# Residual added in PSUM in one unit of fifteen in place of one in six, with a new order of the work: a Restormer block on one Trainium2 core

## The chip, the cores and the metric

The kernel runs on one core of one Trainium2 chip. Its engines are TensorE (PE in the profile, with its weight loads as PEld), VectorE (DVE), ScalarE (ACT), GpSimd (POOL) and SyncE (SP, which issues DMAs). Each works through its own list of instructions in a fixed order, and waits on semaphores for what others make. The metric is the time of one execution on the device in microseconds; of the kernel before there are three timed runs and one profiled execution.

## The reference: what is computed

All numbers are float32. An input of 16 images, 128 channels, 96 x 96 pixels, goes through an attention across channels and a feed-forward part with a 3x3 depthwise convolution, each behind a layer norm and each added to what went in. Cut to what matters:

```python
B, C, H, W = (16, 128, 96, 96); HID = 4 * C; HEADS = 8
def _attention(xn, wq, wk, wv, wp):       # attention of channels on channels, 8 heads of 16
    q, k, v = split(xn @ wq.T), split(xn @ wk.T), split(xn @ wv.T)
    attn = softmax(einsum('bhcn,bhdn->bhcd', l2norm(q), l2norm(k)) * HEAD_DIM ** -0.5)
    ...
    return out @ wp.T
def _ffn(xn, w_in, w_dw, w_out):
    h1 = einsum('bchw,oc->bohw', xn, w_in[:, :, 0, 0])        # 128 -> 512 channels
    h2 = depthwise 3x3 convolution of h1 with w_dw, padding 1
    return einsum('bchw,oc->bohw', gelu(h2), w_out[:, :, 0, 0])
x = x + attn_out                                   # first residual
x = x + _ffn(layernorm(x) over channels, ...)      # second residual: this change is about it
```

## The kernel before, in words

**Tiling.** An image is cut into 8 bands of 12 rows (1152 pixels), a band into 3 units of 4 rows (384 pixels), so that there are 128 bands, counted `g` = 0 to 127, and 384 units. Channels lie on the 128 partitions. An image passes through three stages, and the program runs the first stage of one image, the second of the image before and the feed-forward part at the same time.

- Stage a (norm 1): PE transposes x to pixels on partitions (`forth`, L2072), ACT copies that to a tile `zT` (L2109), DVE takes mean and variance (`stats`, L2080), POOL makes 1/sqrt from them in two small steps (`variance` L2085, `power` L2089) and scales zT with it (`scaled`, L2113). PE sums the Gram matrix over the whole image (L2120) and transposes back to channels (L2168). A chain of small steps turns the Gram matrix into one 128 x 128 matrix for the image.
- Stage b: PE applies that matrix (`mix`, L2022), ACT brings it out of PSUM (L2031), a DMA adds x to it (L2034). Transposes, statistics and `variance`/`power` follow as above, and DVE writes the normalised `xn` (L2172).
- Feed-forward part: for each band the 512 hidden channels are four chunks `n` of 128; a band and chunk together are a job, named (g, n). PE makes the hidden values (`hidden`, L2366) and ACT copies them to SBUF (`kept`, L2371). Of the nine taps of the depthwise convolution ACT makes two to four as separate products (L2382); POOL adds one of these and the middle tap into the tile `merged` (L2385, a second one at L2388); DVE runs the rest as a chain of multiply-adds. The chain begins with a **first tap** that reads `h` and `merged`, both in SBUF (written acc<-h,ratio,merged, L2394), goes on in PSUM (L2398), and ends in the SBUF tile `h3` (h<-h,ratio,acc, L2394). DMAs issued by POOL add the other products on top (L2407, L2410), and ACT applies gelu (L2415). For 45 of the 128 bands the fourth chunk is done by PE alone, as nine matmuls (L2478).
- Output: for each unit PE multiplies the four chunks with `woutT` into one PSUM bank (L2518, two matmul records for each product, since float32 goes through in two passes), the residual x is added, and SP stores the band (L2532).

**The residual.** It is added in one of two ways. Where `in_psum` holds, PE first multiplies x by the identity into the same bank (L2517) and ACT copies the finished sum to SBUF (L2526). Elsewhere DVE adds the bank and x (L2528). `SUM_OF, SUM_AT = 2, 1` says where: unit 1 of every second band, 64 units of 384.

**What sets the order.** `Plan` collects some 18,900 operations with a cost and a due time each; `order()` runs a list scheduler over them, and then moves single operations by hand-searched steps: in `MOVES`, each engine has a table "the operation at place n goes m places later or earlier". So the order on each engine is fixed before the program is built. `in_turn()` replays the lists with a model of durations, to write all engines' operations into one program and to give out buffers. The four PSUM banks `h`, the tiles `zT`, `pr`, `h3`, and the batches of statistics go round among their users; an operation that takes a buffer waits for the last user of it. The replay's times are not on the chip: only its order and its choice of buffers are.

**One port.** The replay treats the first tap on DVE and POOL's `merge` and `scaled` (marked `two`) as taking turns at one port to SBUF.

Of the kernel before, what the change touches and what calls it, by code (L numbers as in the profile page):

```python
# [49 lines left out]
SUM_OF, SUM_AT = 2, 1  # L50
# [164 lines left out]
    PE={6: -1, 11: -1, 13: -1, 18: 0, 19: -3, 26: -1, 28: -1, 29: 7, 33: -3, 37: 3, 38: 6, 39: -4, 44: -2, 47: -2,  # L215
        48: -2, 50: -3, 53: 0, 54: -2, 56: -1, 58: -1, 60: 8, 64: -2, 66: 5, 68: -2, 70: -5, 72: -2, 76: -1,
        78: -1, 84: -1, 88: -1, 90: 0, 91: -2, 95: -1, 102: -7, 105: 0, 106: 5, 107: 7, 108: 1, 110: 6, 111: -9,
        118: -1, 120: 4, 122: -3, 124: -3, 126: 3, 129: 4, 130: -5, 132: 3, 134: 4, 135: -4, 137: 5, 139: 5,
        142: -3, 144: 2, 148: 3, 149: -2, 151: 4, 157: 2, 159: 3, 161: 7, 162: 3, 167: 2, 170: 6, 171: 2, 176: -4,
        177: 2, 179: -5, 180: -3, 185: 2, 194: -3, 196: 7, 197: 5, 199: 9, 200: -22, 203: -23, 204: 7, 206: -23,  # L220
        211: 1, 213: -3, 214: -7, 215: -1, 217: 4, 219: 14, 220: 3, 221: 1, 222: 9, 230: 6, 233: 4, 234: 7, 235: 0,
        238: 1, 239: 9, 241: 9, 242: -8, 243: 2, 246: 12, 250: 4, 254: 18, 255: -31, 256: -30, 257: -28, 258: -28,
        259: -27, 260: -22, 261: -21, 262: -20, 263: -11, 264: -11, 265: -10, 266: -7, 267: -11, 268: -11, 269: -9,
        271: -7, 272: -7, 274: 0, 275: 5, 278: -8, 279: 3, 281: 11, 282: -6, 283: -20, 284: 9, 285: 26, 286: 12,
        287: -18, 288: -15, 289: 24, 290: -19, 294: -15, 295: 2, 296: -15, 297: -9, 298: 17, 301: 17, 305: -1,
        306: -6, 307: 22, 314: -7, 316: -8, 317: -5, 318: 25, 321: 3, 326: 7, 328: -12, 329: 30, 330: 5, 331: -14,
        332: 10, 333: -12, 334: 32, 335: -9, 336: 9, 337: 25, 338: -10, 340: 23, 341: -4, 342: -11, 347: -8,
        348: -1, 349: 15, 356: -1, 357: 10, 358: 10, 359: 11, 360: 9, 361: 11, 362: -14, 363: -13, 371: 17,
        372: -7, 373: -15, 375: -14, 377: 4, 378: 32, 381: 33, 382: -2, 387: 5, 388: -5, 389: -5, 390: -8, 397: 3,
        398: 8, 400: -6, 401: -4, 402: -7, 408: -6, 409: -5, 413: -2, 415: 0, 416: -4, 417: 6, 418: 6, 420: 7,  # L230
        424: -3, 427: 13, 429: -13, 430: 5, 437: 7, 438: 5, 442: -8, 443: -7, 444: -7, 445: 5, 450: 7, 451: 5,
        452: -14, 454: -23, 455: -13, 456: -23, 457: -9, 458: 1, 460: -8, 461: 1, 473: -1, 474: 4, 475: 2, 476: -2,
        477: 37, 478: 37, 479: 6, 480: -1, 481: 35, 484: 33, 486: 4, 487: 6, 488: 6, 491: -3, 496: -1, 498: 5,
        499: 5, 500: -4, 503: 4, 504: 16, 505: 19, 507: 14, 509: 19, 510: 19, 513: 19, 514: 33, 515: -83, 516: -56,
        517: -41, 518: -45, 519: -11, 521: -39, 528: -6, 529: 2, 530: -4, 532: 9, 533: 1, 536: 4, 548: 3, 549: -44,
        550: -41, 552: -27, 554: 12, 555: -44, 557: 1, 558: -5, 560: 2, 561: 8, 562: -7, 563: -9, 565: 13,
        566: -10, 567: -2, 570: 7, 576: 19, 577: 10, 580: 10, 582: 3, 585: -3, 586: -2, 587: -11, 588: -2, 589: 3,
        590: 6, 593: 6, 595: -15, 596: -15, 597: -34, 598: -24, 600: -17, 601: -28, 602: 7, 603: -42, 605: -26,
        606: 8, 608: 8, 609: 8, 610: -8, 614: 4, 616: 9, 618: 23, 620: 8, 621: 2, 624: 0, 633: 0, 636: -1, 637: 0,
        644: 11, 645: 12, 646: 15, 648: 14, 649: 15, 650: 17, 651: 14, 654: 14, 656: 16, 658: 16, 659: -1, 660: 18,  # L240
        661: -57, 662: 8, 663: -31, 666: -18, 668: -12, 670: -17, 671: -21, 673: 7, 675: -4, 676: 30, 677: 32,
        678: 34, 679: 38, 682: -3, 688: 34, 689: -38, 690: 34, 697: 3, 698: 0, 700: -12, 702: 26, 703: 13,
        705: -11, 706: 23, 707: 25, 708: 2, 709: -8, 710: -56, 711: 7, 712: -35, 713: -24, 715: -11, 716: -17,
        717: -14, 719: -12, 720: 0, 727: -8, 730: -4, 733: 5, 734: 3, 735: 4, 740: -5, 749: -3, 750: -1, 751: 5,
        753: 4, 754: 0, 758: 5, 759: 20, 760: 4, 766: -4, 768: -3, 770: -2, 774: -1, 776: 9, 777: 9, 778: 2,
        781: 8, 782: 8, 783: 0, 784: -7, 785: 17, 792: 4, 793: -5, 794: -3, 797: -37, 798: 29, 799: 4, 800: 20,
        801: 0, 802: 5, 804: 0, 810: -4, 813: -4, 815: 2, 817: -7, 818: -5, 819: -7, 820: -4, 821: -6, 822: -8,
        827: 9, 829: -1, 830: 11, 831: 15, 832: -1, 836: 1, 840: -18, 841: 2, 842: -18, 843: -1, 845: -16, 846: -1,
        847: -14, 849: 2, 856: 8, 860: 7, 861: 1, 862: 3, 864: 5, 867: 3, 868: 5, 870: 8, 876: 11, 877: 2, 880: 0,
        883: 5, 885: 5, 887: -38, 888: -38, 889: -41, 890: -29, 891: -34, 892: -26, 893: -1, 896: -2, 897: -1,  # L250
        898: 4, 899: 5, 906: -3, 907: -7, 908: -1, 909: -4, 910: 19, 913: -3, 920: 3, 921: 5, 922: -5, 926: -2,
        930: 0, 934: 0, 942: -5, 945: -6, 947: -5, 948: 4, 949: 10, 950: 3, 951: -37, 953: -2, 955: -17, 957: 18,
        959: -18, 960: 21, 961: 2, 965: 3, 966: 28, 967: -24, 968: 19, 970: -20, 978: -1, 979: 19, 982: -18,
        983: -7, 984: -6, 987: -22, 988: -22, 989: -19, 990: -18, 991: 16, 992: -25, 993: -22, 994: -21, 995: -9,
        996: -22, 997: 4, 998: -10, 999: -20, 1000: 0, 1001: -21, 1002: -20, 1003: 3, 1004: 4, 1005: -22, 1006: 6,
        1007: 4, 1008: 6, 1009: 18, 1010: 10, 1011: 18, 1012: 26, 1013: 26, 1014: 14, 1015: -2, 1016: 1, 1017: 23,
        1018: 25, 1021: 23, 1023: -2, 1024: 23, 1025: 24, 1026: 26, 1027: 6, 1028: 6, 1029: 8, 1030: 23, 1043: -1,
        1044: -19, 1045: -14, 1046: 0, 1048: 36, 1049: 13, 1051: 14, 1053: 46, 1054: 25, 1055: -1, 1056: 24,
        1057: 26, 1060: 27, 1063: -12, 1065: -10, 1068: 21, 1069: -13, 1070: 21, 1071: 21, 1072: -11, 1074: 22,
        1075: -16, 1077: 20, 1079: -22, 1080: 20, 1081: -23, 1083: 18, 1086: -19, 1087: -18, 1089: -19, 1090: -17,  # L260
        1091: 19, 1092: 11, 1093: 12, 1095: -23, 1096: -20, 1097: 12, 1098: -13, 1100: 6, 1101: -24, 1102: -24,
        1103: -28, 1104: -23, 1105: 12, 1106: 8, 1110: 6, 1111: 7, 1112: 8, 1113: 10, 1114: 8, 1115: 20, 1116: 21,
        1117: 7, 1119: 6, 1121: 21, 1122: -9, 1123: 3, 1130: 23, 1132: -5, 1134: -1, 1136: 20, 1140: -2, 1141: -5,
        1142: 50, 1143: 57, 1144: 57, 1145: -13, 1146: -3, 1147: 15, 1148: 16, 1149: 75, 1150: 15, 1151: 64,
        1152: -5, 1153: 65, 1154: -5, 1158: -1, 1168: 8, 1169: 10, 1170: 11, 1173: -21, 1176: -9, 1177: -22,
        1178: -27, 1179: -10, 1180: -10, 1181: -23, 1182: -28, 1183: -11, 1185: 46, 1186: 10, 1187: 12, 1188: 14,
        1190: -10, 1192: -1, 1193: 2, 1194: 52, 1195: -34, 1196: -25, 1197: -24, 1198: -16, 1201: -15, 1202: -13,
        1203: -15, 1204: 22, 1205: 24, 1208: 24, 1209: 18, 1211: 64, 1212: -15, 1215: 22, 1216: 22, 1217: 11,
        1218: -15, 1220: -11, 1221: -10, 1224: 6, 1230: 20, 1231: -17, 1235: 17, 1238: -17, 1240: -18, 1241: -18,
        1243: 20, 1244: -9, 1245: -3, 1247: 33, 1251: 20, 1252: 44, 1253: 44, 1254: 45, 1256: 20, 1257: 24,  # L270
        1258: 42, 1259: 42, 1260: -16, 1262: -14, 1263: 40, 1264: -17, 1265: -7, 1266: -9, 1267: 39, 1268: -9,
        1269: -9, 1275: -7, 1278: -11, 1284: -11, 1285: 22, 1287: -15, 1288: 5, 1289: 20, 1293: -14, 1294: -10,
        1295: -1, 1296: -14, 1299: 31, 1302: -14, 1306: -15, 1307: 9, 1308: 0, 1314: -3, 1316: 1, 1317: -27,
        1318: -26, 1323: -28, 1325: 2, 1326: -28, 1328: -2, 1329: -25, 1330: -28, 1335: -6, 1338: 12, 1339: -5,
        1341: -5, 1342: -5, 1343: -5, 1344: 17, 1345: -17, 1346: 19, 1347: -16, 1348: 11, 1349: 28, 1350: 12,
        1351: -18, 1352: -9, 1353: -9, 1354: -8, 1355: -16, 1356: -16, 1357: 22, 1358: 22, 1359: 23, 1360: 23,
# [2334 lines left out]
```

## Time and profile before

| | |
|---|---|
| timed runs | 3909.78, 3913.20 and 3914.52 us; median 3913.2 |
| profiled execution, its own time | 3910.02 us |
| its span, first to last instruction | 3908.1 us |
| busy, PE / DVE / ACT / POOL | 3852.1 / 3807.1 / 3636.3 / 3370.3 us |
| weight loads, PEld | 2502.7 us |
| granted TensorE clock | 1.000 |

Busy times count an engine's instructions once where they overlap; issuing instructions and waits are not counted. In rows of groups come line, engine, operation, tile written <- tiles read, shape and count, then busy time and the mean of one in ns, then the idle time of the engine just before them and what ended it. In rows of the timeline come start and duration in us, and idle time before the row in brackets.

### The profile page before, as it was taken

To read this page: it belongs to the slowest core of one execution; us is meant where nothing else is said; L and a number is where in the kernel's file an instruction comes from. 1 tells how busy PE (TensorE), PEld (TensorE's weight loads), DVE (VectorE), ACT (ScalarE), POOL (GpSimd) and SP (SyncE) were. 2 spreads that over 40 slices of the span, in tenths; PEclk is the share of its full clock that TensorE was granted. 3 is DMA by queue.
4 is the path that set the end of the run, shared out by engine and by line. 5 is a ranking of instruction groups with operands and counts; after the bars stand their busy time and mean duration, and the time that the engine had idled before them with its cause. 6 is when DMAs were issued, how large, how long until landed. Compare 5 with 4: busy or idle time off the path is not lost.

```text
span 3908.1 us, 50778 instructions
## 1 busy us (share of the span) xinstructions
PE 3852.1 (99%) x16595; PEld 2502.7 (64%) x16595; DVE 3807.1 (97%) x4328; ACT 3636.3 (93%) x5542; POOL 3370.3 (86%) x3107
## 2 busy tenths in 40 slices
PE   8999999999999999999999999999999999999999
PEld 7666666666666666666666666666666666666555
DVE  7999999999999999999999999999999999999998
ACT  3999999999999999999999999999999999999996
POOL 5998888888898888989889899898998889888784
PEclk9999999999999999999999999999999999999999
DMA  3999999999999999999999999999999999999996
GB/s 99 191 206 213 196 209 204 209 200 201 200 200 204 206 192 210 200 210 210 192 204 204 202 210 201 206 200 212 206 204 199 210 211 189 213 207 187 203 192 146
DMA packets 191689, 777.39 MB, mean 199 GB/s; under 512 B 22208, under 2 KB 23616, under 8 KB 191424
## 3 DMA queue, kind: packets, MB, share of 16 engines
q0 software_dynamic: 151920, 622.33, 83.9%
q1 hardware_dynamic: 38784, 151.75, 10.7%
q8 instruction: 131, 2.15, 0.2%
q14 instruction: 134, 1.10, 0.1%
q10 hardware_dynamic: 720, 0.07, 0.0%
HBM read 148.85 MB, written 75.50 MB: 57 GB/s over the span
## 4 chain that ended last, share of the span: by engine, by line
PE 38%; DVE 5%; ACT 3%; POOL 2%; issue 1%; DMA 1%; POOLq 0%; DVEq 0%; ACTq 0%
PE h L2518 11%; PE h L2366 9%; PE h L2478 8%; PE h L2022 2%; PE h L2168 2%; PE g L2120 2%; PE h L2072 2%; DVE acc L2398 2%; ACT pr L2382 1%; DVE acc L2394 1%; DVE h L2394 1%; POOL merged L2385 1%; ACT h L2415 1%; ACT h L2371 1%; DMA h<-pr 1%
## 5 line engine op out<-in xcount | busy, mean ns | idle before, releaser
L2382 ACT ACTIVATE pr<-h,ratio 128x1152 f32<-128x1152 f32 x1494 | 1847.7, 1267 | 17.8 <-DMA h<-pr 5.5
L2398 DVE SCALAR_TENSOR_TENSOR acc<-h,ratio,acc 128x1152 f32<-128x1152 f32 (+1 forms) x1308 | 1809.7, 1384 | 11.3
L2385 POOL TENSOR_TENSOR merged<-pr,h 128x1152 f32<-128x1152 f32 x466 | 1207.8, 2592 | 110.2 <-DVE acc L2394 56.8
L2518 PE MATMUL h<-h,woutT 128*128 128x384 f32 x3072 | 1115.2, 486 | 1.9 <-ACT h L2492 1.2
L2366 PE MATMUL h<-xn,winT 128*128 128x384 f32 (+2 forms) x2802 | 1097.8, 494 | 14.0 <-DVE x L2528 3.7
L2478 PE MATMUL h<-xn,comp 128*128 128x380 f32 (+2 forms) x2430 | 902.8, 482 | 0.1
L2518 PEld LDWEIGHTS h<-h,woutT 128*128 128x128 f32 x3072 | 563.1, 189 | 353.6 <-issue 13.3
L2371 ACT COPY h<-h 128x384 f32<-128x384 f32 (+2 forms) x1401 | 658.3, 493 | 81.8 <-PE h L2366 76.1
L2394 DVE SCALAR_TENSOR_TENSOR acc<-h,ratio,merged 128x1152 f32<-128x1152 f32 x466 | 684.1, 1468 | 15.6 <-POOL merged L2388 7.9
L2366 PEld LDWEIGHTS h<-xn,winT 128*128 128x128 f32 x2802 | 495.9, 190 | 309.4 <-issue 22.6
L2394 DVE SCALAR_TENSOR_TENSOR h<-h,ratio,acc 128x1152 f32<-128x1152 f32 x467 | 655.4, 1403 | 5.9
L2410 POOL DMA_DIRECT2D h<-pr x466 | 475.0, 1030 | 175.7 <-PE h L2518 23.5
L2415 ACT ACTIVATE h<-h,ksum 128x1152 f32<-128x1152 f32 (+1 forms) x586 | 611.9, 1070 | 13.1 <-DMA h<-pr 12.4
L2478 PEld LDWEIGHTS h<-xn,comp 128*128 128x128 f32 x2430 | 429.5, 189 | 223.4 <-issue 14.3
L2407 POOL DMA_DIRECT2D pr<-pr x466 | 469.6, 1026 | 74.9 <-ACT pr L2382 58.7
L2089 POOL TENSOR_TENSOR ve_b<-ve_b,mhalf 128x4 f32<-128x4 f32 x288 | 356.5, 1256 | 10.7
L2072 PEld LDWEIGHTS h<-ident,x 128*128 128x128 f32 x2244 | 270.5, 141 | 134.1 <-issue 57.8
L2089 POOL TENSOR_TENSOR ve_a<-ve_a,mhalf 128x4 f32<-128x4 f32 x288 | 346.5, 1208 | 10.5
L2113 POOL TENSOR_TENSOR zT<-zT,ve_a 128x512 f32<-128x512 f32 x270 | 344.2, 1283 | 5.8
L2072 PE MATMUL h<-ident,x 128*128 128x128 f32 x2244 | 331.5, 274 | 9.7 <-DMA x<-in_x_dram 2.4
L2022 PE MATMUL h<-xn,mwT 128*128 128x384 f32 x768 | 296.5, 489 | 5.2 <-DVE st_b L2080 1.9
L2120 PEld LDWEIGHTS g<-zT 128*128 128x128 f32 x2160 | 273.1, 191 | 42.7 <-POOL zT L2113 4.6
(190 smaller groups left out, 3940.2 us busy)
## 6 DMA issues: line engine op xcount, KB each, us to landing
pr<-pr POOLq DMA_DIRECT2D x466, 576.0 KB, 7.1
h<-pr POOLq DMA_DIRECT2D x466, 576.0 KB, 7.6
x<-in_x_dram SPq DMA_DIRECT2D x128, 576.0 KB, 6.5
out_dram<-x SPq DMA_DIRECT2D x127, 576.0 KB, 4.6
x<-in_x_dram POOLq DMA_DIRECT2D x123, 576.0 KB, 7.7
out_dram<-x SPq DMA_DIRECT2D x3, 192.0 KB, 1.9
h<-in_L_conv_w_in_dram SPq DMA_DIRECT2D x1, 256.0 KB, 3.3
h<-in_L_conv_w_out_dram SPq DMA_DIRECT2D x1, 256.0 KB, 3.7
```

Source lines behind the costliest of these rows:

```text
L2072: nc.tensor.transpose(d["pT", q][:, k, :], xt[:, j * P : (j + 1) * P], ident)
L2089: nc.gpsimd.tensor_tensor(rstd, rstd, mhalf, ALU.pow)
L2366: nc.tensor.matmul(rows(ph), lhsT=winT[:, n, :], rhs=window(xn, r0 + r, e - r, 1), start=True, stop=True)
L2371: nc.scalar.copy(window(h1_, r, e - r, 1), rows(d.pop(("ph", r))))
L2382: nc.scalar.activation(to, shifted(t), AF.Copy, scale=ratio[:, n, t : t + 1])
L2385: nc.gpsimd.tensor_tensor(merged, d["pr", dma_taps[0]], shifted(UNIT), ALU.add)
L2394: nc.vector.scalar_tensor_tensor(to, shifted(t), ratio[:, n, t : t + 1], also, ALU.mult, ALU.add)
L2398: nc.vector.scalar_tensor_tensor(to, shifted(t)[:, lo:hi, cut], ratio[:, n, t : t + 1], to, ALU.mult, ALU.add)
L2410: nc.gpsimd.dma_start(out=h3_of(g, n), in_=d["pr", dma_taps[1]], accum_op=ALU.add)
L2415: nc.scalar.activation(h3, h3, AF.Gelu, bias=ksum[:, z, n : n + 1])
L2478: nc.tensor.matmul(d["pc"][:, lo:hi, cut], lhsT=comp[:, t, :], rhs=window(xn, r0 + dy, UR, dx)[:, lo:hi, cut], start=(t == order[0]), stop ...
L2518: nc.tensor.matmul(rows(d["po"]), lhsT=woutT[:, n, :], rhs=h3s[g, n][:, s * UR : (s + 1) * UR, :], start=(k == 0 and not in_psum), stop=(k ...
```

## The change

Three things change.

1. `SUM_OF` goes from 2 to 5. `in_psum` now holds for unit 1 of every fifth band: 26 units in place of 64. Of the 64, 13 stay; 51 go to DVE's add, and 13 others go from DVE to PE and ACT. Net, 38 units lose the identity product on PE and the copy on ACT, and get an add on DVE.
2. `in_turn()` has more of a model: after a DMA issue POOL's next results come later (`LAG`, `ISSUED`), and a first tap on DVE that comes within `RACE` of certain starts on POOL lets a POOL operation with a port turn go ahead of it. `PE_RATE` goes from 0.989 to 1.002.
3. Nearly every row of `MOVES` is new. Counted over the operations that stay on their engine, 66% of PE's, 37% of DVE's, 73% of ACT's and 61% of POOL's stand at another place; the median of the shift is one place or none, and nine in ten move by at most two to four.

```diff
-SUM_OF, SUM_AT = 2, 1
+SUM_OF, SUM_AT = 5, 1
...
-    PE={6: -1, 11: -1, 13: -1, 18: 0, 19: -3, 26: -1, 28: -1, 29: 7, 33: -3, 37: 3, 38: 6, 39: -4, 44: -2, 47: -2,
...
-PE_RATE, SPARE = 0.989, 75
+PE_RATE, SPARE, LAG, ISSUED, RACE, AHEAD = 1.002, 75, 300, 250, 940, 560
...
         dma = port = taken = 0.0
+        lag, behind = 0, -RACE
...
                     if e == "POOL" and not ops[k][8]:
                         time = max(time, taken)
+                    if e == "DVE" and ops[k][9] and time < behind + RACE and head["POOL"] < len(lists["POOL"]):
+                        other = lists["POOL"][head["POOL"]]
+                        if ops[other][9]:
+                            if times.get("POOL") is None:
+                                times["POOL"] = ready(other, "POOL")
+                            if times["POOL"] is not None and times["POOL"] <= min(time + AHEAD, free_at["POOL"] + 40):
+                                time = max(time, times["POOL"] + 1)
...
             if engine == "POOL":
                 last_pool = None if queue else k
+                straight = time < free_at["POOL"] + 40
+                behind = time if queue else time + ns - 600 if straight and two else -RACE
+                lag = 2 if queue else lag if straight else 0
+                if queue:
+                    ns -= ISSUED
+                elif lag:
+                    result += LAG * lag / 2
+                    lag -= 1
```

The changed file has 7 lines more ahead of the functions, so that each line number above is 7 higher in it (L2528 is L2535 there).

**First place: DVE, band 62** (band 6 of image 7; x_7_6 is its residual). The add of unit 1 was not on DVE; rows run in DVE's order. Before:

```order
L2394 SCALAR_TENSOR_TENSOR h_1_154<-h_2_142,ratio,acc 128x1152
L2528 TENSOR_TENSOR x_7_6_12661<-h_76,x_7_6_12661 128x384
L2394 SCALAR_TENSOR_TENSOR acc<-h_3_143,ratio,merged 128x1152
L2172 TENSOR_TENSOR xn<-x_8_1_13295,h_74 128x4x96
L2398 SCALAR_TENSOR_TENSOR acc<-h_3_143,ratio,acc 128x1056
L2080 BN_STATS st_a_8_13593<-zT_161 128x6
L2398 SCALAR_TENSOR_TENSOR acc<-h_3_143,ratio,acc 128x1056
L2528 TENSOR_TENSOR x_7_6_12661<-h_76,x_7_6_12661 128x384
L2398 SCALAR_TENSOR_TENSOR acc<-h_3_143,ratio,acc 128x1056
```

The same place on DVE in the changed kernel:

```order
L2401 SCALAR_TENSOR_TENSOR h_1_154<-h_2_142,ratio,acc 128x1152
L2535 TENSOR_TENSOR x_7_6_12644<-h_73,x_7_6_12644 128x384
L2401 SCALAR_TENSOR_TENSOR acc<-h_3_143,ratio,merged 128x1152
L2405 SCALAR_TENSOR_TENSOR acc<-h_3_143,ratio,acc 128x1056
L2535 TENSOR_TENSOR x_7_6_12644<-h_76,x_7_6_12644 128x384
L2405 SCALAR_TENSOR_TENSOR acc<-h_3_143,ratio,acc 128x1056
L2535 TENSOR_TENSOR x_7_6_12644<-h_75,x_7_6_12644 128x384
L2179 TENSOR_TENSOR xn<-x_8_1_13283,h_73 128x4x96
L2405 SCALAR_TENSOR_TENSOR acc<-h_3_143,ratio,acc 128x1056
```

Two adds of this band have become three, between the taps of one chain, and the write of xn stands later.

**Second place: POOL, band 76** (the job that begins image 9's fifth band; ve_a is the 1/sqrt of stage a, merged<-pr,h the merge). Before, in POOL's order:

```order
L2385 TENSOR_TENSOR merged<-pr_151,h_0_140 128x1152
L2388 TENSOR_TENSOR merged<-merged,pr_149 128x1152
L2085 TENSOR_SCALAR ve_a_0_15994<-st_a_0_15944 128x4
L2407 DMA pr_150<-pr_145 128x1152
L2113 TENSOR_TENSOR zT_164<-zT_164,ve_a_17_15969 128x4x128
L2089 TENSOR_TENSOR ve_a_0_15994<-ve_a_0_15994,mhalf 128x4
L2385 TENSOR_TENSOR merged<-pr_151,h_1_141 128x1152
```

The same place on POOL in the changed kernel:

```order
L2092 TENSOR_SCALAR ve_a_0_15944<-st_a_0_15929 128x4
L2392 TENSOR_TENSOR merged<-pr_145,h_0_140 128x1152
L2120 TENSOR_TENSOR zT_164<-zT_164,ve_a_17_15922 128x4x128
L2395 TENSOR_TENSOR merged<-merged,pr_150 128x1152
L2096 TENSOR_TENSOR ve_a_0_15944<-ve_a_0_15944,mhalf 128x4
L2392 TENSOR_TENSOR merged<-pr_152,h_1_141 128x1152
```

The scaling of zT stood behind both merges and a DMA issue; it now stands between the two merges, and the DMA issue has gone further back.

More of the change, by code (lines that the diff above doesn't have):

```diff
@@ L214 @@
 MOVES = dict(
-    PE={6: -1, 11: -1, 13: -1, 18: 0, 19: -3, 26: -1, 28: -1, 29: 7, 33: -3, 37: 3, 38: 6, 39: -4, 44: -2, 47: -2,
[320 rows of a table removed]
-    DVE={2: -1, 8: 0, 9: -2, 12: -1, 16: -1, 18: -1, 19: 2, 24: -2, 32: 0, 34: 5, 36: 6, 37: -6, 38: -2, 40: -5,
[161 rows of a table removed]
-    ACT={5: -1, 7: -1, 9: 3, 12: -2, 13: 3, 16: 5, 20: -1, 22: -4, 25: 2, 33: -2, 39: -1, 41: 2, 42: 3, 43: 5,
[275 rows of a table removed]
-    POOL={0: 5, 2: 4, 4: 5, 5: 18, 6: 5, 7: 19, 18: -3, 21: -3, 28: -1, 30: -2, 32: -1, 38: 0, 40: -4, 42: -3,
[147 rows of a table removed]
-    SP={8: -5, 17: -1, 20: -1, 22: -1, 24: -1, 30: -1, 32: -1, 34: -1, 37: -2, 40: -1, 44: -1, 46: -1, 50: -1,
[4 rows of a table removed]
@@ L1127 @@
-    h={18: -1, 23: 1, 24: -1, 25: -3, 28: -1, 30: 7, 33: -2, 36: 0, 37: -2, 38: -4, 40: -2, 43: -1, 48: -1,
[164 rows of a table removed]
-    x1={22: -1},
-    h3={0: 6, 15: -1, 26: -1, 38: -1, 49: -1, 73: -1, 85: -2, 97: -2, 120: -1, 134: -1, 145: -1, 158: -1, 168: -1,
-        181: -2, 193: -1, 205: -1, 218: -1, 231: -3, 241: -1, 254: -1, 265: -1, 278: -1, 290: -2, 313: -2, 327: -3,
-        337: -1, 348: -1, 361: -1, 373: -1, 386: -1, 396: -1, 409: -1, 469: -1, 480: -1, 492: -1, 502: -1, 507: -2,
-        514: 2, 520: -1},
+    PE={3: -3, 10: 3, 12: -5, 16: 3, 19: -2, 21: 7, 26: -2, 27: 3, 29: 6, 32: 4, 33: -8, 38: 6, 39: 1, 40: -1,
[320 rows of a table added]
@@ new lines @@
+    DVE={2: 0, 4: 1, 5: -5, 7: -3, 9: -1, 11: -1, 14: 0, 16: 0, 19: -6, 21: -1, 29: -1, 31: 3, 35: 1, 37: -6, 39: 0,
[160 rows of a table added]
+    ACT={2: -2, 5: -2, 6: -2, 9: -1, 14: -1, 16: 6, 19: -1, 22: -1, 24: -8, 25: 2, 29: 4, 32: -1, 33: -4, 39: -1,
[269 rows of a table added]
+    POOL={2: 4, 4: 4, 5: 21, 6: 5, 7: 21, 9: -7, 11: -7, 13: -4, 20: -5, 30: -1, 32: -2, 37: 4, 39: 3, 41: 2, 43: 2,
[144 rows of a table added]
+    SP={1: -1, 5: 0, 7: 0, 8: -6, 17: -1, 20: -1, 22: -1, 36: 0, 37: -2, 46: -1, 48: -1, 52: -1, 57: 0, 58: -2,
[3 rows of a table added]
+    h={4: -1, 6: 3, 10: -3, 14: 1, 15: -4, 17: -3, 22: -2, 23: 3, 28: -1, 30: 8, 33: -1, 35: 4, 36: -3, 40: 0,
[166 rows of a table added]
@@ L1297 @@
+    x1={1: -1, 4: -1, 22: -1},
+    xb={1: -1},
+    h3={2: -1, 4: -2, 6: -1, 15: -2, 26: -1, 38: -1, 73: -1, 85: -2, 96: -1, 109: -1, 134: -1, 145: -1, 168: -1,
+        181: -2, 193: -2, 205: -1, 231: -3, 254: -1, 265: -1, 278: -2, 289: -1, 301: -1, 313: -2, 327: -3, 337: -2,
+        361: -2, 373: -1, 386: -1, 409: -1, 480: -1, 492: -2, 502: -2, 515: -1, 519: -1},
 )
 ISSUE, FROM_POOL, PORT = dict(DMA=500, DVE=480, ACT=240), 170, 126
-PE_RATE, SPARE = 0.989, 75
+PE_RATE, SPARE, LAG, ISSUED, RACE, AHEAD = 1.002, 75, 300, 250, 940, 560
```

2133 rows, old and new, of tables (ACT, DVE, PE, POOL) are left out of this document.

## The prediction

> **What bounds the kernel now.** I read the page's first part, then the stretches of the span, then the waits of the fullest engine, and last the timeline where a term has to be priced.
>
> ```profile
> PE 3852.1 (99%) x16595; PEld 2502.7 (64%) x16595; DVE 3807.1 (97%) x4328; ACT 3636.3 (93%) x5542; POOL 3370.3 (86%) x3107
> PE 38%; DVE 5%; ACT 3%; POOL 2%; issue 1%; DMA 1%; POOLq 0%; DVEq 0%; ACTq 0%
> ```
>
> Two engines are nearly full: PE, with 3908.1 - 3852.1 = 56.0 us idle, and DVE, with 101.0 us. The chain that ended last names PE far more than DVE. The change takes work from the first and gives work to the second, so the question is how much room DVE has. The stretches tell where its idle time lies (after the stretch come PE, PEld, DVE, ACT and POOL, busy us and instructions):
>
> ```profile
> 0.00:100.00 100.00, 88.21 (x580) 71.86 (x581) 74.54 (x190) 36.39 (x73) 58.52 (x113) 1.00 0.35 102
> 100.00:3850.00 3750.00, 3709.37 (x15845) 2398.50 (x15844) 3693.07 (x4105) 3572.99 (x5420) 3299.76 (x2985) 1.00 0.97 203
> 3850.00:3909.00 59.00, 54.55 (x173) 32.34 (x171) 39.51 (x35) 26.90 (x50) 12.05 (x11) 1.00 0.52 121
> ```
>
> Of DVE's 101.0 us, 25.5 lie in the first 100 us, 18.6 after 3850, and 56.9 in the 3750 us between. There DVE is 98.5% busy and PE 98.9%: both bound it, each waiting a little for the other.
>
> The end cannot give much:
>
> ```profile
> 3886.19 1.42 DVE L2394 SCALAR_TENSOR_TENSOR h<-h,ratio,acc 128x1152 f32<-128x1152 f32 x1
> ...
> 3903.94 1.20 DVE L2528 TENSOR_TENSOR x<-h,x 128x384 f32<-128x384 f32 x2 [9.90 <-PE h L2518]
> ```
>
> DVE's last tap ends at 3887.6, and 20.5 us follow in which PE finishes the output. In the order, 24 products on PE stand from the first that needs this last tap to the end, before and after the change alike. So I take those 20.5 us as fixed: the end comes when DVE has got through its taps, plus 20.5. PE's saving reaches the end only through DVE's waits.
>
> **The change part by part.** All sums are made against the profiled execution's own time, 3910.0 us (span 3908.1, 1.9 around it). It is 3.2 below the median of the three runs and inside their range.
>
> *Work moved, 38 units net.* What one unit costs on each engine:
>
> ```profile
> 1999.19 0.81 PE L2517 MATMUL h<-x,ident 128*128 128x384 f32 x2
> 1999.84 1.45 PE L2518 MATMUL h<-h,woutT 128*128 128x384 f32 x4
> ...
> L2526 ACT COPY x<-h 128x384 f32<-128x384 f32 x64 | 30.9, 483 | 3.6 <-PE h L2518 3.3
> ...
> 2004.14 0.55 DVE L2528 TENSOR_TENSOR x<-h,x 128x384 f32<-128x384 f32 x1
> 2004.61 1.42 DVE L2394 SCALAR_TENSOR_TENSOR acc<-h,ratio,merged 128x1152 f32<-128x1152 f32 x1
> ```
>
> Records overlap, so I take the distance from one start to the next. PE: 0.65 us for the two identity records, 38 x 0.65 = **24.7 us less**. ACT: 38 x 0.483 = 18.4 us less; ACT has 272 us idle, so this counts for nothing. DVE: 0.47 us for an add, 38 x 0.47 = **17.9 us more**, and with DVE 98.5% full nothing hides it.
>
> An add on DVE also adds a wait: the taps queued behind it stand still until PE has finished the unit, and PE gets the bank back from DVE in place of ACT. Rows of the middle stretch price both:
>
> ```profile
> L2528 DVE TENSOR_TENSOR x<-h,x 128x384 f32<-128x384 f32 x311 | 170.8, 549 | 5.3 <-PE h L2518 4.1 <-issue 0.4
> L2366 PE MATMUL h<-xn,winT 128*128 128x384 f32 (+2 forms) x2758 | 1080.6, 494 | 13.8 <-DVE x L2528 3.7 <-DVE xn L2172 3.1 <-ACT h L2371 1.7
> ```
>
> 5.3 us for 311 adds makes 0.65 for 38, and 3.7 on PE makes 0.45; I leave both out. The band's store on SP waits for the add wherever it is made, so no queue but DVE's is passed.
>
> *Port turns.* First taps read `h` and `merged`, both in SBUF; last taps of the same size read PSUM for one of the two:
>
> ```profile
> L2394 DVE SCALAR_TENSOR_TENSOR acc<-h,ratio,merged 128x1152 f32<-128x1152 f32 x461 | 676.7, 1468 | 15.2 <-POOL merged L2388 7.9 <-POOL merged L2385 5.3
> L2394 DVE SCALAR_TENSOR_TENSOR h<-h,ratio,acc 128x1152 f32<-128x1152 f32 x461 | 646.9, 1403 | 5.8
> ```
>
> The difference, 676.7 - 646.9 = 29.8 us, is time in which first taps stand still. It sits in few of them. 21 took over 1.65 us; these are the longest, the shortest, and one that shows with POOL's rows how it comes about:
>
> ```profile
> 1003.86 4.20 DVE L2394 SCALAR_TENSOR_TENSOR acc<-h,ratio,merged 128x1152 f32<-128x1152 f32 x1
> 2876.86 1.67 DVE L2394 SCALAR_TENSOR_TENSOR acc<-h,ratio,merged 128x1152 f32<-128x1152 f32 x1
> ...
> 2370.58 0.91 POOL L2407 DMA_DIRECT2D pr<-pr  x1
> 2371.23 1.34 POOL L2113 TENSOR_TENSOR zT<-zT,ve_a 128x512 f32<-128x512 f32 x1
> 2372.24 2.42 POOL L2089 TENSOR_TENSOR ve_a<-ve_a,mhalf 128x4 f32<-128x4 f32 x1
> ...
> 2370.84 2.96 DVE L2394 SCALAR_TENSOR_TENSOR acc<-h,ratio,merged 128x1152 f32<-128x1152 f32 x1
> ```
>
> While POOL issued a DMA (2370.58) the tap started (2370.84), the scaling of zT got in first all the same, and the tap took 2.96 us in place of some 1.40. The new order takes this scaling away from there (second place above): it runs between the two merges, for which the tap has to wait anyway. In 20 of the 21 a scaling stood on POOL behind the tap's own last merge, straight or with small steps between, or behind a DMA issue that follows that merge. In the new order 4 of the 20 have lost this pattern and 16 keep it; whether those still collide hangs on a few hundred ns, which no order shows. Over the whole list, 85 scalings stand straight behind a DMA issue, and 82 did before, so new losses can arise. Bounds: 0 and 29.8 us. The 4 places alone would make 4/20 of 29.8, 6.0; a list that moved at six places in ten on POOL should shift others too. I take half, **14.9 us less**.
>
> *Waits of DVE in the middle.* The longest, of the 56.9 us:
>
> ```profile
> DVE xn L2172 <- PE h L2168: 8.2, 15, 1.8
> DVE acc L2394 <- POOL merged L2388: 7.9, 7, 3.0
> DVE acc L2394 <- POOL merged L2385: 5.3, 9, 1.4
> DVE x L2528 <- PE h L2518: 4.1, 11, 0.8
> DVE st_b L2080 <- PE h L2072: 3.8, 8, 0.9
> ```
>
> 16.1 us are waits for PE, 13.2 for POOL's merge. PE gets 24.7 us of room, so its results come earlier against DVE's list: between 0 and 16.1, I take 10. The merge comes late where it stands behind a DMA issue or a port turn; the replay now reckons with that, but 265 merges stand straight behind a DMA issue where 230 did. Between 0 and 13.2, I take half, 6.6. The other 27.6 us of DVE's idle time are gaps of well under a microsecond, and I leave them. Nothing excludes that a new order makes new waits; the rivals price that.
>
> **The sum.** 3910.0 + 17.9 - 14.9 - 10 - 6.6 = **3896.4 us**, 13.6 less than now. PE then has 24.7 - 13.6 = 11.1 us more idle time than now, which fits an engine that is no longer the first bound. With nothing regained it is 3910.0 + 17.9 = 3927.9; with all three terms in full (59.1 together), 3910.0 + 17.9 - 29.8 - 16.1 - 13.2 = 3868.8.
>
> **The rivals.**
>
> *DVE alone is the bound, and the new order wins nothing (slower).* DVE pays 17.9 us in the middle stretch, its port losses only move to other taps, and PE waits longer: 3927.9 us. It comes out slower by over 0.2% (above 3921.0 against the median) when less than 7 us come back of the 59.1 that could. For it: DVE has just 56.9 us idle in 3750, and as many scalings stand behind DMA issues as before. Against it: the chain that ended last follows PE for 38% of the span and DVE for 5%. The Trainium skill has a rule by which this rival would be the rule: Perfetto Trace Analysis, section "Identifying the Most-Contended Engine", says that the busy share of matmuls is no measure of how near the limit PE is, and that the share of the weight loads is to be taken instead. By that, PE stands at 64% and DVE at 97%, the work taken from PE is worth nothing, and the sum is 3927.9 less whatever the order regains. This trace does not bear the rule out in full:
>
> ```profile
> 2363.88 3.23 PE h L2518 x10
> ```
>
> Ten records start 0.32 us apart here, and the 0.65 us from one unit's identity product to its next record is the same pace: PE does not idle behind its 64%. Chance 0.17.
>
> *The order wins about what the adds cost.* Between 7 and 23 of the 59.1 us come back and the time is near 3911 (3905 to 3921). This is also the case in which the table does not do what its model says, since the replay is a model and only its order reaches the chip. Chance 0.23.
>
> *PE was the bound.* Then its saving comes through in full, 3910.0 - 24.7 = 3885.3 us, and port turns that are won come on top as far as DVE's list allows: near 3877 (3869 to 3885). For it: PE's share of the chain, and PE idle only 40.6 us in the middle. Against it: DVE would have to regain 51 of its 59.1 us. Chance 0.16.
>
> **How the numbers follow.** The forecast, some half of DVE's losses regained (3885 to 3905), has 0.44; the three rivals have, in their order, 0.17, 0.23 and 0.16. A measurement of this kernel can tell about 0.2% from no change, that is 7.8 us at 3913.2: faster is below 3905.4, slower above 3921.0. So faster 0.44 + 0.16 = 0.60, same 0.23, slower 0.17. The range runs from 3873 to 3922: it takes in the forecast, the case of no change and the first of the slower one, and most of the case in which PE was the bound. It leaves out some 0.15 above and 0.04 below.
>
> **What would show it.** In the changed profile: the identity products x52, DVE's adds x358 and ACT's copies x26; DVE's busy time at 3807.1 + 17.9 - 14.9 = 3810 us and PE's some 3840 (its records overlap, and it stays close to full); the mean of first taps near 1435 ns where it is 1468; waits of DVE for PE in the middle near 6 us and for the merge near 7; DVE's last tap some 14 us earlier, and still about 20 us from there to the end. The prediction is wrong if first taps still average 1468 or more, if DVE's idle time in the middle stays at 57 us or grows, or if the 20 us of the end change.

## The result, and the profile after

| | before | after |
|---|---|---|
| timed runs, median | 3911.5 us (4 runs, 3907.9 to 3914.5) | 3938.3 us (4 runs, 3934.0 to 3942.3) |
| ratio, 95% interval | | 1.0069 [1.0051, 1.0086] |
| profiled execution, its own time | 3910.0 us | 3942.3 us |
| DVE idle in the middle stretch | 56.9 us | 76.9 us |
| PE idle in the middle stretch | 40.6 us | 70.9 us |

The change makes the kernel 26.8 us slower. The forecast was 3896.4 us, 41.9 below the measured time, and the measured time lies above the range of 3873 to 3922. The first part and the chain of the page after:

```profile
PE 3855.6 (98%) x16519; PEld 2482.2 (63%) x16519; DVE 3819.4 (97%) x4366; ACT 3625.7 (92%) x5504; POOL 3414.2 (87%) x3107
PE 38%; DVE 14%; POOL 10%; issue 5%; ACT 3%; DMA 2%; POOLq 0%; DVEq 0%; ACTq 0%
```

GpSimd (POOL) executes the same 3107 instructions as before, is busy 43.9 us longer, and its share of the chain goes from 2% to 10%. The stretches follow, with the columns as before. The program grew by 32 us, so the middle stretch is taken 30 us longer and the last one 2 us:

```profile
0.00:100.00 100.00, 89.60 (x584) 72.27 (x585) 73.75 (x189) 35.61 (x70) 55.93 (x112) 1.00 0.35 100
100.00:3880.00 3780.00, 3709.08 (x15760) 2376.47 (x15759) 3703.15 (x4142) 3560.69 (x5382) 3344.34 (x2985) 1.00 0.96 201
3880.00:3941.00 61.00, 56.93 (x180) 33.48 (x178) 42.49 (x37) 29.43 (x54) 13.98 (x11) 1.00 0.58 131
```

The loss is in the middle: DVE's idle time there is 3780.0 - 3703.15 = 76.9 us, PE's 3780.0 - 3709.08 = 70.9 us. PE has 76 records less to work through and is idle longer. The last tap and the last add show that the end is as it was:

```profile
3919.01 1.41 DVE L2401 SCALAR_TENSOR_TENSOR h<-h,ratio,acc 128x1152 f32<-128x1152 f32 x1
...
3937.03 0.56 DVE L2535 TENSOR_TENSOR x<-h,x 128x384 f32<-128x384 f32 x1 [0.66 <-PE h L2525]
```

The last tap ends at 3920.4, 32.8 us later than before, and 20.2 us follow where 20.5 did. The counts are as the change says (PE shows two records for each of the 26 identity products):

```profile
L2524 PE MATMUL h<-x,ident 128*128 128x384 f32 x52 | 21.0, 485 | 0.0
L2533 ACT COPY x<-h 128x384 f32<-128x384 f32 x26 | 12.4, 477 | 4.1 <-PE h L2525 4.1
L2535 DVE TENSOR_TENSOR x<-h,x 128x384 f32<-128x384 f32 x358 | 197.2, 552 | 19.1 <-PE h L2525 18.5
```

Next, taps of the middle stretch, and under them DVE's longest waits in it:

```profile
L2401 DVE SCALAR_TENSOR_TENSOR acc<-h,ratio,merged 128x1152 f32<-128x1152 f32 x461 | 671.1, 1456 | 26.3 <-POOL merged L2392 13.5 <-POOL merged L2395 10.6
L2401 DVE SCALAR_TENSOR_TENSOR h<-h,ratio,acc 128x1152 f32<-128x1152 f32 x461 | 648.6, 1407 | 5.7
```

```profile
DVE acc L2401 <- POOL merged L2392: 13.5, 18, 2.2
DVE xn L2179 <- PE h L2175: 11.3, 17, 1.8
DVE acc L2401 <- POOL merged L2395: 10.6, 11, 2.2
DVE st_b L2087 <- PE h L2079: 7.3, 10, 2.4
DVE x L2535 <- PE h L2525: 4.6, 4, 2.2
```

First taps lose 671.1 - 648.6 = 22.5 us in place of 29.8. DVE waits 24.1 us for the merge in place of 13.2, and in the three rows for PE 4.6 + 11.3 + 7.3 = 23.2 in place of 16.1. Put into the prediction's sum that makes 3910.0 + 17.9 - 7.3 + 7.1 + 10.9 = 3938.6, near the 3942.3 of this execution. But such a sum only says where DVE stood still; what made it stand still is for the runs to tell.

GpSimd's own groups, before and then after:

```profile
L2385 POOL TENSOR_TENSOR merged<-pr,h 128x1152 f32<-128x1152 f32 x466 | 1207.8, 2592 | 110.2 <-DVE acc L2394 56.8 <-ACT pr L2382 38.3 <-ACT h L2415 4.6
L2089 POOL TENSOR_TENSOR ve_b<-ve_b,mhalf 128x4 f32<-128x4 f32 x288 | 356.5, 1256 | 10.7
L2089 POOL TENSOR_TENSOR ve_a<-ve_a,mhalf 128x4 f32<-128x4 f32 x288 | 346.5, 1208 | 10.5
```

```profile
L2392 POOL TENSOR_TENSOR merged<-pr,h 128x1152 f32<-128x1152 f32 x466 | 1255.9, 2695 | 111.6 <-DVE acc L2401 56.3 <-ACT pr L2389 43.7 <-ACT h L2378 2.6
L2096 POOL TENSOR_TENSOR ve_a<-ve_a,mhalf 128x4 f32<-128x4 f32 x288 | 393.0, 1368 | 8.9
L2096 POOL TENSOR_TENSOR ve_b<-ve_b,mhalf 128x4 f32<-128x4 f32 x288 | 379.4, 1333 | 9.8
```

The same instructions take longer: `power` 772.4 us in place of 703.0, the first merge 1255.9 in place of 1207.8. Of the 48 us more in the merge, some 42 lie in merges that start without a gap behind a DMA issue of GpSimd. By the two traces these are 108 before, of 2.80 us on average, and 165 after, of 2.92; a merge that starts behind a pause lasts 2.43 in both. And PE waits longer for `power` (`ve_b`) and for the scaling (`zT`), here before and then after:

```profile
PEld h L2168 <- POOL ve_b L2089: 10.3, 20, 1.8
PEld g L2120 <- POOL zT L2113: 4.6, 9, 1.2
PE h L2168 <- POOL ve_b L2089: 2.2, 4, 1.3
```

```profile
PEld h L2175 <- POOL ve_b L2096: 25.3, 36, 2.3
PEld g L2127 <- POOL zT L2120: 11.5, 17, 1.7
PE h L2175 <- POOL ve_b L2096: 10.9, 14, 1.8
```

Summed over all rows of the view of waits, PE, PEld, DVE and ACT wait 43 us for GpSimd before and 109 us after. PE and PEld are one engine, and some of its waits stand in the rows of both: taken once, its part is 22 us before and 48 after. Of ACT's part after, 13.1 us are one wait in the first 100 us. One place of after shows how a result comes late, in GpSimd's and DVE's timelines:

```profile
1091.24 0.88 POOL L2414 DMA_DIRECT2D pr<-pr  x1
1091.86 1.75 POOL L2096 TENSOR_TENSOR ve_a<-ve_a,mhalf 128x4 f32<-128x4 f32 x1
1093.59 0.91 POOL L2417 DMA_DIRECT2D h<-pr  x1
1094.20 1.19 POOL L2414 DMA_DIRECT2D pr<-pr  x1
1094.76 2.69 POOL L2120 TENSOR_TENSOR zT<-zT,ve_a 128x512 f32<-128x512 f32 x2
1096.76 3.08 POOL L2392 TENSOR_TENSOR merged<-pr,h 128x1152 f32<-128x1152 f32 x1
...
1099.87 1.43 DVE L2401 SCALAR_TENSOR_TENSOR acc<-h,ratio,merged 128x1152 f32<-128x1152 f32 x1 [2.23 <-POOL merged L2392]
```

Three DMA issues, a `power` of 1.75 us, two scalings and a merge of 3.08 us follow one another without a gap, and DVE stands still for 2.23 us until the merge is done.

### The profile page after: what moved, and what is told of

It reads as the page before. It is cut to its first block, busy times and chain, and to the rows that moved or that the text cites. A ratio compares the mean times of both kernels' runs of the same rounds, so it can differ in the third digit from the quotient of the medians.

```text
span 3940.6 us, 50578 instructions
## 1 busy us (share of the span) xinstructions
PE 3855.6 (98%) x16519; PEld 2482.2 (63%) x16519; DVE 3819.4 (97%) x4366; ACT 3625.7 (92%) x5504; POOL 3414.2 (87%) x3107
## 4 chain that ended last, share of the span: by engine, by line
PE 38%; DVE 14%; POOL 10%; issue 5%; ACT 3%; DMA 2%; POOLq 0%; DVEq 0%; ACTq 0%
PE h L2525 9%; PE h L2373 9%; PE h L2485 8%; DVE acc L2405 6%; PE h L2029 3%; DVE acc L2401 3%; POOL merged L2392 3%; PE h L2175 3%; PE g L2127 3%; PE h L2079 2%; DVE h L2401 2%; ACT pr L2389 1%; DMA h<-pr 1%; POOL merged L2395 1%; POOL ve_a L2096 1%
## 5 line engine op out<-in xcount | busy, mean ns | idle before, releaser
L2392 POOL TENSOR_TENSOR merged<-pr,h 128x1152 f32<-128x1152 f32 x466 | 1255.9, 2695 | 111.6 <-DVE acc L2401 56.3
L2417 POOL DMA_DIRECT2D h<-pr x466 | 494.1, 1075 | 150.4 <-issue 17.7
L2414 POOL DMA_DIRECT2D pr<-pr x466 | 500.0, 1086 | 77.0 <-ACT pr L2389 58.1
L2096 POOL TENSOR_TENSOR ve_a<-ve_a,mhalf 128x4 f32<-128x4 f32 x288 | 393.0, 1368 | 8.9
L2096 POOL TENSOR_TENSOR ve_b<-ve_b,mhalf 128x4 f32<-128x4 f32 x288 | 379.4, 1333 | 9.8
L2120 POOL TENSOR_TENSOR zT<-zT,ve_a 128x512 f32<-128x512 f32 x270 | 363.2, 1363 | 5.4
```

The costliest lines, as they stand in the source:

```text
L2096: nc.gpsimd.tensor_tensor(rstd, rstd, mhalf, ALU.pow)
L2392: nc.gpsimd.tensor_tensor(merged, d["pr", dma_taps[0]], shifted(UNIT), ALU.add)
L2414: nc.gpsimd.dma_start(out=d["pr", dma_taps[1]], in_=d["pr", t], accum_op=ALU.add)
```

## The experiments

"Before" in each ratio is the kernel before, timed beside the run. Where a run takes one kernel's order with other units, the operations that change engine stand where the replay of that order puts them; no search has fitted them in. Line numbers of the experiments' kernels differ from the two above.

**Units and order apart.** The first run has the old order and the new units, the second the new order and the old units.

```diff
-SUM_OF, SUM_AT = 2, 1      # old MOVES, old replay
+SUM_OF, SUM_AT = 5, 1
```

> The order of before, with the 51 adds that move to VectorE and the 13 that move to TensorE and ScalarE put where the old replay had them. Theory U (the moved adds cost it: 17.9 us of VectorE's time, and PSUM banks held until VectorE comes to them; the new order is neutral): 3930 to 3940 us, near the changed kernel's 3938, and TensorE's waits for L2528 near 30 us. Theory O (the new order loses the time, the adds little): 3908 to 3920 us.

```diff
-SUM_OF, SUM_AT = 5, 1      # new MOVES, new replay
+SUM_OF, SUM_AT = 2, 1
```

> The order of after, with the residuals summed in PSUM in one unit of six as before. Theory U: back to 3908 to 3918 us. Theory O: 3925 to 3938 us, with TensorE and VectorE waiting for GpSimd as in the changed kernel (some 65 and 25 us).

Measured: units only 3927.2 us, ratio 1.0049 [1.0032, 1.0065]; order only 3958.2, 1.0130 [1.0115, 1.0145]. Neither part wins anything. The first time lies between the ranges of the two theories, the second above both. The units cost 18.3 us (before, beside it, 3908.8), as if the prediction's 17.9 had come in full. The new order with its own units is another 11 us above, which the two intervals do not quite tell apart; with the old units it costs 49.

**Buffers or order.** `in_turn()` also decides which buffer and bank each tile gets. This run keeps after's lists word for word and lets the old replay hand out the buffers.

> Every engine's order as in after, and the sums as in after; only the replay is the old one, so that some operations get other buffers and PSUM banks. If the choice of buffers matters, the time moves by more than 8 us from the changed kernel's 3938; if it doesn't, as theories U and O both have it, within 6 us of it.

Measured: 3943.0 us, 1.0084 [1.0069, 1.0099], beside 1.0069 for the change itself, whose interval overlaps. The buffers do not carry the loss; the lists do.

**GpSimd's list.** Three runs rearrange it alone. In the first, each of the 288 merges that stand straight behind a DMA issue in the list (265 first ones and 23 second ones) goes ahead of that issue; in the second, the changed kernel takes GpSimd's list of before; in the third, the old order with the new units takes GpSimd's list of after.

```diff
 POOL's list, 288 places
-DMA issue, merge
+merge, DMA issue
```

> After, but on GpSimd each of the 288 merges that stand straight behind a DMA issue goes ahead of that issue. Theory L (merges come late because they stand behind DMA issues, and VectorE's first taps wait for them): waits of VectorE for merged fall from 24 to under 12 us, and the time from 3938 to 3920 to 3930. Rival (GpSimd is late as a whole, and a DMA issued 2.5 us later is late too): 3936 or more, with more time lost waiting for DMAs.

> The changed kernel, with GpSimd's list alone taken from the order of before (7 of its 3072 operations have to stand elsewhere, or the lists would block each other). Theory P (the new order loses its time on GpSimd: its results come later against the other lists): below 3933 us, toward the 3927 of e1, and the waits of TensorE and VectorE for GpSimd fall from 91 toward 40 us. Rival M (no single list is at fault; lists that were searched together fit one another): 3945 us or more.

> e1 (old order, units as after), with GpSimd's list alone taken from the new order (7 operations elsewhere). Theory P: 3935 to 3945 us, the time of the changed kernel, with some 90 us of waits for GpSimd. Rival M: 3945 us or more, clearly above the changed kernel, as e7.

Measured: 4032.0 us, 1.0315 [1.0300, 1.0331]; 4058.2, 1.0384 [1.0364, 1.0403]; 4084.1, 1.0452 [1.0435, 1.0469]. The first was meant to take away the issues' delay of the merges and lost 94 us: a DMA issued one merge later lands later, and ACT's waits for DMAs rise to 98 us (21 with the change). So the run shows what a later issue costs, and leaves open what the merges lose behind the issues. The other two show that GpSimd's list fits the lists beside it: exchanged alone, it costs 120 and 157 us. They cannot say which list is to blame.

**What a unit costs, in the old order.** The prediction priced a unit by DVE's 0.47 us. Four runs take the exchange apart. The first leaves the identity product out in the 51 units and changes nothing else (the residual is missing there). The second lets DVE add those 51 and keeps the product on PE (the residual is in twice there). The third lets DVE add them with the product gone, as the change does. The fourth only moves the 13 other units from DVE to PE and ACT.

```diff
+        summed = in_psum and g % 5 == 0          # first run: the order of before
-                if in_psum:
+                if summed:
                     nc.tensor.matmul(d["po"], lhsT=ident, ...
```

> Before, in the old order, but the identity product is left out in the 51 units that the change takes from TensorE (their residual is missing from the output); ScalarE's copy stays, and VectorE gets nothing. TensorE loses 51 x 0.65 = 33 us of work. If VectorE sets the end (theory V): 3899 to 3909 us, little of it comes through. If TensorE does: 3872 to 3885 us.

> Before, in the old order, with those 51 units added on VectorE as well (51 x 0.47 = 24 us) in place of ScalarE's copy, and TensorE's identity product kept (the residual goes in twice there). Theory V: the adds come through in full, 3930 to 3936 us, and taking 24.7 us from TensorE in e1 brought next to nothing. If TensorE's saving paid for part of the adds in e1: 3942 us or more.

> Old order; the same 51 units as in the run with the adds alone are added by DVE, and here their identity product is left out as it should be (the output is the reference's); the 13 other units stay on PE and ACT and none moves the other way. Theory A (PE's saving is worth nothing, and the 8 us by which the units alone, 3927.2, stand above the adds alone, 3919.6, come from the 13 units that moved the other way): as with the adds alone, 3919 to 3922. Rival B (with the product gone PE reaches its waits for DVE's adds sooner and loses the time there and more, so that the 8 us belong to the product's absence): 3927 or more.

> Old order; nothing changes but that the 13 units that the change moves from DVE to PE and ACT are moved (identity product and ACT copy added, DVE's add gone), the 64 others stay. Theory A (these 13 are what makes the units alone, 3927.2, dearer than the 51 adds alone, 3917.7): about 8 us slower than before, 3916 to 3920, though DVE gets 6.1 us less work. Rival C (DVE's work sets the price of a unit, as in the prediction's 0.47 us for each; the 8 us come from how the two moves together fit): 3904 to 3912, no slower than before.

| run | work moved | median us | ratio |
|---|---|---|---|
| product left out | PE -33 us | 3909.0 | 1.0008 [0.9999, 1.0017] |
| 51 adds, product kept | DVE +24, ACT -25 us | 3919.6 | 1.0027 [1.0017, 1.0038] |
| 51 adds, product gone | DVE +24, ACT -25, PE -33 us | 3917.7 | 1.0026 [1.0016, 1.0035] |
| 13 units the other way | DVE -6, ACT +6, PE +8 us | 3917.6 | 1.0025 [1.0014, 1.0035] |

The work moved is reckoned from the prediction's costs of one unit; PE's busy time itself fell by 18.5 us in the first run, 3852.1 to 3833.6. The 33 us of PE's work are worth nothing in the old order, taken away alone or together with the adds: PE was 99% busy, and the ratio is 1.0008. DVE's three waits for PE in the middle stretch hardly change in the first run, 15.1 us where 16.1 stood. The Trainium skill's rule that was weighed in the prediction (Perfetto Trace Analysis, section "Identifying the Most-Contended Engine") says that the busy share of matmuls is no good measure of how near its limit PE is. The old order agrees with it, by the ratio of 1.0008. The 51 adds cost 8 to 10 us, not 24, below both ranges of the run with the product kept. The 13 units cost 10 us although DVE gets 6 us less to do. The last two rows make +0.26% and +0.25%, together about the 0.49% of the units alone. So the 18 us were not 38 adds of 0.47 us; the size fits by accident. Part of the 8 and the 10 us may come from where the replay puts the moved operations, which no run separates.

**GpSimd's lateness by itself.** After the first merge, `power` takes the most of GpSimd's busy time: 1.2 to 1.4 us on average, 576 times. In these runs it is a multiplication, so that what follows is no longer scaled by 1/sqrt; every list stays as it is.

```diff
-                nc.gpsimd.tensor_tensor(rstd, rstd, mhalf, ALU.pow)
+                nc.gpsimd.tensor_tensor(rstd, rstd, mhalf, ALU.mult)
```

> The changed kernel with `power` on GpSimd (576 instructions, 1.2 to 1.4 us each in the profiles) done as one multiplication in place of a power; what it computes there is no longer 1/sqrt. It goes with the two runs below, where the same is done to the old order. Theory T (the new order loses because GpSimd's results come later: waits of PE, DVE and ACT for GpSimd are 109 us here and 38 us with the old order and the same units): with a lighter GpSimd these waits fall to under 40 us and the distance to the old order with the same units (now 3938.3 - 3927.2 = 11 us) shrinks to under 4, so about 3925. Rival S (the new order loses where PE, DVE and ACT meet each other, and GpSimd's lateness is only seen along the way): the distance stays at 8 us or more, about 3935. If the multiplication takes as long as the power, the waits stay and the run tells nothing.

> Old order with the changed units (one in five bands), `power` done as one multiplication. Both theories: GpSimd's waits are only 38 us there, so between 3915 and 3927 (3927.2 with the power). T: the changed kernel with the same edit stands less than 4 us above; S: 8 us or more above.

> The kernel before, `power` done as one multiplication. T and S alike: GpSimd's lateness costs the old order little (waits for it sum to 43 us over all engines, few of them on the path), so a gain of 0 to 12 us, 3898 to 3910. If it gains over 20 us, GpSimd is a bound already before the change, and a term of the prediction that is worked out from DVE's room alone is mis-sized.

> New order with the units of before (one in six), `power` on GpSimd done as one multiplication in place of a power (no 1/sqrt there). With the power this pair stood at 3958.2, 20 us above the changed kernel. Theory D (DVE is the bound once GpSimd is not late, and PE's load is worth nothing): fewer adds on DVE make it faster than the changed kernel with the same edit (3897.2), by up to the 15 us that the units cost in the old order with this edit (3923.7 - 3908.9), so 3882 to 3895. Rival E (the new order lives on the room that PE gets from fewer identity products): it stands above 3897.2 by 8 us or more, so over 3905.

| order, units | GpSimd as it is | with light `power` |
|---|---|---|
| old, old (before) | 1 | 3908.9 us, 0.9998 [0.9988, 1.0008] |
| old, new | 3927.2 us, 1.0049 [1.0032, 1.0065] | 3923.7 us, 1.0042 [1.0027, 1.0057] |
| new, new (after) | 3938.3 us, 1.0069 [1.0051, 1.0086] | 3897.2 us, 0.9969 [0.9957, 0.9981] |
| new, old | 3958.2 us, 1.0130 [1.0115, 1.0145] | 3929.1 us, 1.0055 [1.0040, 1.0070] |

Of the changed kernel with the light `power` follow the first part of the page, one of the two rows of `power`, DVE's first taps, and waits for GpSimd:

```profile
PE 3838.2 (99%) x16519; PEld 2476.4 (64%) x16519; DVE 3809.1 (98%) x4366; ACT 3620.3 (93%) x5504; POOL 2897.7 (74%) x3107
```

```profile
L2096 POOL TENSOR_TENSOR ve_a<-ve_a,mhalf 128x4 f32<-128x4 f32 x288 | 121.5, 425 | 8.9
...
L2401 DVE SCALAR_TENSOR_TENSOR acc<-h,ratio,merged 128x1152 f32<-128x1152 f32 x466 | 674.2, 1447 | 8.5 <-POOL merged L2395 4.8 <-POOL merged L2392 1.8
```

```profile
DVE acc L2401 <- POOL merged L2395: 4.8, 4, 1.8
PEld h L2175 <- POOL ve_b L2096: 3.3, 8, 1.3
DVE acc L2401 <- POOL merged L2392: 1.8, 3, 0.7
```

The old order is 1 and 4 us faster for it, little beside the new order's 29 and 41. With the new units the new order then stands 26.5 us below the old, where it stood 11 above; waits for GpSimd, summed over the rows as above, are 18 us in place of 109. The new order thus pays for GpSimd's time, and the old order does not. The theory had expected 3925 for after; the size was too small. How much of the 26.8 us comes from the 43.9 us by which GpSimd got busier the runs do not show, since the light `power` takes off far more, 516.5 us (3414.2 to 2897.7).

**And PE behind it.** The old units cost 32 us in the new order with the light `power` (3929.1 against 3897.2), so its time could hang on PE's room. Two runs put the identity product back on PE in the 51 units, beside DVE's adds (residual twice there), and touch no list.

```diff
+        summed = in_psum or s == SUM_AT and g % 2 == 0 and g < NG - 1
-                if in_psum:
+                if summed:
```

> The changed kernel with `power` as one multiplication (3897.2 us), and with the identity product put back on PE in the 51 units from which the change takes it, while DVE's adds stay: the residual is in twice there, and PE gets 51 x 0.65 = 33 us more work, no other engine any. Rival E (behind a light GpSimd the new order lives on PE's room): 20 to 33 us slower, 3917 to 3930. Theory D (PE's load is worth nothing, and the 32 us by which the old units stand above in the new order come from adds that don't fit that order): within 6 us, 3894 to 3903.

> The changed kernel as it is, with `power` as a power (3938.3 us), and with the identity product put back in the same 51 units beside DVE's adds: residual twice there, 33 us more work on PE. If PE's room is taken up by GpSimd's late results in any case (E under a late GpSimd), it gives little: under 8 us, 3936 to 3946. If PE is the bound there too, 20 us or more, over 3958.

> The changed kernel with those 13 units given back to DVE (the residual in PSUM only in unit 1 of every tenth band, 13 units in all; the new order otherwise). Theory A carried over: 5 to 10 us faster than the changed kernel (3938.3), 3928 to 3933. Rival C: DVE gets 6.1 us more, 3938 to 3946. Theory D and rival E of the run above: PE gets 8.5 us less work, so E expects it faster as A does, D no faster.

Measured: with the light `power` 3914.2 us, 1.0015 [1.0005, 1.0024], 17 us above; with the real one 3950.6, 1.0107 [1.0092, 1.0122], 12 us above (18 and 15 by the ratios). So 33 us of PE's work cost about half of themselves in the first and some 0.4 in the second, where they were worth nothing in the old order. What the prediction drew from the rule of the Trainium skill, that work taken from PE is worth nothing, does not hold in the new order. Both times lie between the ranges of the two theories: the new order does lean on PE's room, and the other 15 of the 32 us lie in the rest of the exchange (DVE's adds, ACT's copies, the 13 other units), which no run takes apart. The 13 units given back (3939.4 us, 1.0083 [1.0068, 1.0098]) make no difference that the intervals can tell in the new order, so their 10 us belong to the old order, not to the units.

## Why the prediction was wrong

- **The bound.** "The end comes when DVE has got through its taps, plus 20.5" held: 20.2 us. Nothing contradicts that PE's saving reaches the end only through DVE's waits. But in the old order 33 us less work on PE took 1.0 of the 16.1 us off these waits and nothing off the time, where the sum had 10.
- **Work moved, 17.9 us: right size, wrong cause.** The units alone cost 18.3. But 51 adds cost 8 to 10 us, 13 units less on DVE cost another 10, and DVE's 0.47 us for an add decides neither. "With DVE 98.5% full nothing hides it" is refuted: with 51 adds more and the product gone, DVE is busy 19.5 us longer (3826.6) and the kernel takes 8 us longer.
- **Port turns, 14.9 us less: 7.3.** First taps do lose less, 1456 ns where 1435 was expected and 1468 stood. So half of the gain came. The reckoning stopped at DVE. While first taps lose 7.3 us less, `power` takes 69 us more in its rows and the first merge 48; whether part of this is turns handed on to GpSimd, no run shows.
- **Waits for POOL's merge, 6.6 us less: 10.9 more**, and **waits for PE, 10 less: 7.1 more.** This is the step that failed. The bounds of both terms were nothing and the whole of the wait that was there, so that a wait could only shrink, though the prediction itself says that "Nothing excludes that a new order makes new waits". GpSimd stood in the sum only as the one that DVE waits for at the merge. That PE waits for GpSimd's `power` and scalings, and DVE then for PE, was not in it. With the light `power` the waits for GpSimd fall from 109 to 18 us, DVE's three waits for PE in the middle from 23.2 to 14.1, and the time by 41 us. The prediction's own sign of being wrong, DVE's idle time in the middle at 57 us or more, came in at 76.9.
- **The rivals.** The sign came from *DVE alone is the bound* (3927.9), but its mechanism did not: DVE has room for over half of the adds in the old order, and the new order does not merely win nothing, it pays for GpSimd. A rival that ends on GpSimd was missing. A sign of it stood in the prediction, 265 merges straight behind a DMA issue where 230 did, and was read only as a smaller gain; the merges behind issues do take most of the merge's 48 us, but that they make the loss is not shown.
- **What would have been right.** With the light `power` the changed kernel shows most of the forecast's numbers: 3897.2 us (3896.4), DVE busy 3809.1 (3810), PE 3838.2 (3840), 6.6 us of waiting for the merge (7), first taps 1447 ns (1435). DVE's three waits for PE in the middle (100 to 3840 us) are 14.1 us, where near 6 was forecast. The fit of the total is luck in part, since that kernel does not do the same work; but it shows that a gain of the expected size is there when GpSimd has less to do.

Two things stay open: which of GpSimd's delays (port turns, issues ahead of a step, the order of its steps) makes most of the loss, and why either move of units costs the old order some 10 us. No version that computes the reference and beats the kernel before came out of these runs.

## What to carry to other kernels

When the order changes on four engines at once, price each term from both sides, also for the engine that is off the chain: an engine with 14% idle time that serves three others can come to hold them up when the places of its steps change. Ask what a saving is worth by leaving the work out in the kernel before; here one such run (33 us of PE, ratio 1.0008) would have cast doubt on the 10 us that the sum took from DVE's waits for PE. It would not have settled them, since in the new order PE's work did count. And where a forecast's size comes out right, take its cause apart all the same: 18.3 us matched 17.9, and the reason given for it did not hold.

## What was not expected of the hardware

- The records of the same GpSimd instructions are longer in another order: `power` 1.21 and 1.26 us on average before, 1.37 and 1.33 after, with single ones above 3 us, as these two, of which the second starts 1.02 us after the first:

```profile
2580.13 3.13 POOL L2096 TENSOR_TENSOR ve_b<-ve_b,mhalf 128x4 f32<-128x4 f32 x1
2581.15 3.09 POOL L2096 TENSOR_TENSOR ve_a<-ve_a,mhalf 128x4 f32<-128x4 f32 x1
```

- The second starts 1.02 us behind the first while both last 3.1 us. In the kernel before, the `power` at 2364.31 lasts 1.03 us, and the next instruction starts 1.02 us after it. So by the records the engine takes the next instruction at the same pace, and these two results come some 2 us later. Spans on GpSimd are rough.
- A merge of GpSimd that starts without a gap behind its own DMA issue lasts 2.80 us (before) and 2.92 us (after) on average, and 2.43 us behind a pause.
- DMA issues placed one merge (2.43 us and more) later, at 288 places, cost 94 us.
